# The scan's carried state columns copied by GpSimd instead of ScalarE, in a selective-scan and mixture-of-experts kernel

## The chip, the cores and the metric

One core of a Trainium2 chip runs the kernel. The metric is device time in microseconds for one execution, smaller being better. The engines are named as in the profile: PE (TensorE, with its weight loads as PEld), DVE (VectorE), ACT (ScalarE), POOL (GpSimd) and SP (SyncE, which issues most DMAs). Each engine takes its instructions strictly in the order of its own queue and waits at each one for the semaphores that it needs.

## The reference

Inputs are two sequences of 2048 tokens of 256 numbers, all float32. Everything starts from a layer norm of x. Two branches follow, and their product is added to x:

```python
xn = layernorm(x)
s = mamba_block(xn)            # a selective scan, then an MLP of width 1024
g = silu(moe(xn))              # 8 experts, the top 2 of each token
return x + s * g
```

The part that matters here is the scan. With 512 channels, 16 states per channel, and B and C computed from the input:

```python
def step(h, ts):
    dt_t, B_t, C_t, u_t = ts
    dA = exp(dt_t[..., None] * A)
    h = h * dA + (dt_t * u_t)[..., None] * B_t[:, None, :]
    y = einsum('bds,bs->bd', h, C_t)
    return h, y
```

The state h is carried from each token to the next over the whole sequence.

## The kernel before, in words

The 4096 tokens are cut into 8 blocks of 512; blocks 0 to 3 are the first sequence, 4 to 7 the second. Channels lie on the 128 partitions, in four groups d = 0 to 3, and the 16 states are taken two at a time, g = 0 to 7. So the scan has 256 steps, in the order of block c, group d, pair g; step n is 32c + 8d + g. One step works on tiles of 128 x 2 x 512 and goes through five engines' queues:

- ACT: two exponentials (L1254) make the decays `da` of the step, two steps ahead. `da` has three buffers.
- DVE: for g = 0 the product `du` of the time step and the input (L1358); for each step the product with B (L1361, into PSUM) and two scans over 512 tokens (L1365), one for each state. Their first value is zero in the first block of a sequence and otherwise a column of `hs` of the block before. The scans write `h`, which has five buffers.
- A copy of the last columns of the two scans (128 x 2) into `hs`, for the scan of the next block (`save`, L1291). It is done for blocks 0 to 2 and 4 to 6, 192 steps in all; blocks 3 and 7 end a sequence and save nothing. Before the change ACT does it.
- POOL: the product with C, in place in `h` (L1295), and for most steps the sum of the two states (L1297).
- PE: adds the result into the accumulator `y` in PSUM by a matmul with the identity (L1267), three steps late.

Because L1295 overwrites `h` in place, it has to wait until the copy has read its columns. The loop issues the copy and the product of step n - 1 after the first scan of step n:

```python
if q == 0 and n > 0:
    save(n - 1)
    times_c(n - 1)
exps(n + LEAD, q)
```

`times_c` issues L1295 and L1297, `exps` issues L1254.

All other work is put between the steps by a planner written out in the kernel. `draw` hands out pieces of PE work worth about 2 us for each half step (projections, the next block's front, the experts and, later, the MLP), and a queue of postponed work (`later`) puts the ACT, DVE and POOL instructions that follow from them one or more half steps later. Nothing of it is decided at run time: the order of each engine's queue is fixed when the kernel is built. The parts that come into the prediction's steps are:

- the front of the next block, softplus for a channel group: ACT does L629, L630, L632, L634, L635, POOL subtracts (L636), ACT takes the logarithm (L643), POOL finishes with L648 and L649. In blocks after the first, two groups at a time.
- `root`, for an earlier block's rms norm: POOL L800, ACT L802 and L803, POOL four small operations on 128 x 4 (L227 to L230). It is issued between the two L643 of the first pair of groups.
- the experts: PE matmuls L854 into `phe`, relu on ACT (L954) into `hide`, PE matmuls L866 into `poe`. ACT also copies the transposed rows of the next expert (L846).
- the MLP of finished blocks, from block 5 on: the same matmul lines into `phm` and `pom`, ACT L1018 and L1026, DVE L1028. For its gate POOL gathers expert rows by indirect DMAs (L1058) and adds them (L1076), ACT takes a tanh (L1080), DVE multiplies (L1083, L1101, L1102).
- in block 0 POOL also issues the indirect DMAs that scatter token rows to the experts (L459).

Of the kernel before, what the change touches and what calls it, by code (L numbers as in the profile page):

```python
# [19 lines left out]
T = 512  # L20
# [29 lines left out]
def kernel(  # L50
# [18 lines left out]
    nc = tc.nc  # L69
# [1142 lines left out]
    hs, ys, y_n, hts, das, dus = {}, {}, {}, {}, {}, {}  # L1212
# [75 lines left out]
    def save(n):  # L1288
        c, d, g = at[n]
        if c % CPB != CPB - 1:  # L1290
            nc.scalar.copy(hs[c][:, d, 2 * g : 2 * g + 2], hts[n][:, :, T - 1])  # L1291

    def times_c(n):
        c, d, g = at[n]
# [41 lines left out]
    for n in range(NS):  # L1336
        c, d, g = at[n]
# [14 lines left out]
        for q in range(2):  # L1352
# [17 lines left out]
# [3 lines that stand above are left out]
# [4 lines left out]
            if q == 0:  # L1377

                past = n - BACK
                if past >= 0 and at[past][1] == ND - 1 and at[past][0] + 1 < NBLK:  # L1380
                    load_bc(at[past][0] + 1, at[past][2])
            owed = draw(HALF + owed)
    save(NS - 1)
    times_c(NS - 1)
    for n in range(NS - LAG, NS):
# [64 lines left out]
```

## Time and profile before

| | |
|---|---|
| median of 3 runs | 1550.95 us (1548.26 to 1552.72) |
| the profiled execution | 1551.53 us |
| its span, first to last instruction | 1549.8 us |
| mean granted TensorE clock | 0.948 |
| busy ACT, DVE, POOL | 919.8, 1244.3, 1154.8 us |
| copy L1291 on ACT | 192 of them, 0.188 us each |
| L1295, L1297 on POOL | 2.38 and 1.29 us each |

A row of the profile's groups names line, engine, operation, output and inputs with their shapes, how often, then busy time in us and the mean in ns, and then the idle time of the engine just ahead of these instructions with what ended most of it. The timeline has one row for each instruction or run of equal instructions: start in us from the span's beginning, length, engine, line, and in brackets the idle time ahead of it and what ended it. The first scan of blocks 1 to 4 starts at 272.4, 440.4, 609.5 and 774.

### The profile page before, as it was taken

What the parts mean: (1) busy time and instruction counts of PE and PEld (TensorE: products, weight loads), DVE (VectorE), ACT (ScalarE), POOL (GpSimd) and SP (SyncE); (2) the same over time, 40 slices, a digit from 0 to 9 for tenths busy, and PEclk for the clock granted to TensorE, in tenths of its full rate; (3) what the DMA queues carried; (4) which work ended last, traced back from release to release, by engine and by line L of the source; (5) the groups of instructions that cost most, each with busy time, mean ns of one, the idle gap of its engine ahead of it and who ended that gap; (6) DMA issues with size and microseconds to landing.
All of it is one profiled execution on the core that took longest, in us unless ns stands there. A gap on an engine that the chain in (4) does not pass through costs nothing. (4 is left out here: it accounts for less than half of the span.)

```text
span 1549.8 us, 18158 instructions
## 1 busy us (share of the span) xinstructions
PE 1396.0 (90%) x5246; PEld 982.9 (63%) x5246; DVE 1244.3 (80%) x1362; ACT 919.8 (59%) x1890; POOL 1154.8 (75%) x775
## 2 busy tenths in 40 slices
PE   6747999998999999999999999999888988899667
PEld 4524677666676577667766777667555656667436
DVE  7558887797788977799879777986898788899942
ACT  4846676575656764477557655676465664475322
POOL 2777689768786689679977897688865778677741
PEclk9558999999999999999999999999998999999888
DMA  5594347723592438524853467345610125412100
GB/s 188 206 378 162 94 141 250 268 86 110 165 343 86 129 115 288 199 87 144 271 214 118 129 217 283 92 125 186 225 48 27 49 68 208 131 35 68 55 14 28
DMA packets 171108, 233.70 MB, mean 151 GB/s; under 512 B 19824, under 2 KB 141552, under 8 KB 171008
## 3 DMA queue, kind: packets, MB, share of 16 engines
q1 hardware_dynamic: 164864, 215.75, 42.0%
q0 software_dynamic: 6144, 16.79, 3.2%
q8 instruction: 42, 0.69, 0.2%
q14 instruction: 58, 0.48, 0.1%
HBM read 196.04 MB, written 36.44 MB: 150 GB/s over the span
## 5 line engine op out<-in xcount | busy, mean ns | idle before, releaser
L1295 POOL TENSOR_TENSOR h<-h,C 128x1024 f32<-128x1024 f32 x256 | 608.7, 2379 | 230.9 <-ACT hs L1291 187.4
L1365 DVE TENSOR_TENSOR_SCAN h<-da,hs,b 128x512 f32<-128x512 f32 x384 | 479.0, 1271 | 42.7 <-PE y L1267 17.6
L1254 ACT ACTIVATE da<-dt,a_neg 128x512 f32<-128x512 f32 x512 | 358.2, 718 | 41.6 <-DVE h L1365 41.2
L1267 PE MATMUL y<-h,ident 128*128 128x512 f32 x594 | 304.9, 616 | 32.4 <-POOL h L1295 18.3
L1361 DVE TENSOR_TENSOR b<-du,B 128x1024 f32<-128x1024 f32 x256 | 314.7, 1229 | 19.3 <-DMA B<-bcd 13.3
L854 PE MATMUL phe<-xsTe,w_e 128*128 128x256 f32 x1248 | 290.8, 385 | 13.5 <-ACT hide L954 8.9
L854 PEld LDWEIGHTS phe<-xsTe,w_e 128*128 128x128 f32 x1248 | 239.1, 192 | 81.5 <-issue 25.6
L866 PE MATMUL poe<-w_e,hide 128*128 128x256 f32 x1248 | 289.2, 380 | 0.0
L1297 POOL TENSOR_TENSOR h<-h 128x512 f32<-128x512 f32 x215 | 276.4, 1286 | 16.9
L866 PEld LDWEIGHTS poe<-w_e,hide 128*128 128x128 f32 x1248 | 236.0, 191 | 65.1 <-issue 33.6
L954 ACT ACTIVATE hide<-phe,b 128x256 f32<-128x256 f32 x312 | 129.3, 469 | 129.3 <-PE phe L854 129.1
L1267 PEld LDWEIGHTS y<-h,ident 128*128 128x128 f32 x594 | 112.9, 197 | 122.9 <-issue 66.0
L1365 DVE TENSOR_TENSOR_SCAN h<-da,b 128x512 f32<-128x512 f32 x128 | 151.2, 1210 | 11.2 <-PE y L1267 3.2
L854 PE MATMUL phm<-xsTm,w_m 128*128 128x256 f32 x512 | 125.2, 397 | 21.4 <-DVE hidm L1028 20.8
L854 PEld LDWEIGHTS phm<-xsTm,w_m 128*128 128x128 f32 x512 | 100.6, 198 | 48.9 <-DVE hidm L1028 25.9
L866 PE MATMUL pom<-w_m,hidm 128*128 128x256 f32 x512 | 122.0, 390 | 3.1 <-DVE xom L1102 3.0
L866 PEld LDWEIGHTS pom<-w_m,hidm 128*128 128x128 f32 x512 | 100.0, 197 | 31.8 <-issue 14.4
L1291 ACT COPY hs<-h 128x2 f32<-128x2 f32 x192 | 36.1, 188 | 99.6 <-DVE h L1365 99.4
L459 POOL DMA_INDIRECT xs_d<-xt,slot x64 | 63.3, 989 | 38.7 <-DVE scratch L441 19.8
L1058 POOL DMA_INDIRECT yk<-ys_d,row_y x64 | 61.6, 962 | 38.6 <-DVE pom L1101 21.3
L582 DVE SCALAR_TENSOR_TENSOR xc<-px,par_sb,xc 128x512 f32<-128x512 f32 x96 | 71.5, 746 | 16.6 <-ACT xc L574 11.7
L966 DVE TENSOR_TENSOR ys<-poe,b 128x512 f32<-128x512 f32 x39 | 26.6, 682 | 58.8 <-PE poe L866 51.9
(175 smaller groups left out, 1438.3 us busy)
## 6 DMA issues: line engine op xcount, KB each, us to landing
w_e<-in_w SPq DMA_DIRECT2D x312, 256.0 KB, 3.5
B<-bcd SPq DMA_DIRECT2D x64, 512.0 KB, 6.9
C<-bcd SPq DMA_DIRECT2D x64, 512.0 KB, 7.3
xs<-xs_d SPq DMA_DIRECT2D x39, 256.0 KB, 2.7
ys_d<-ys SPq DMA_DIRECT2D x39, 256.0 KB, 4.2
b<-in_b SPq DMA_DIRECT2D x39, 128.0 KB, 4.1
xnr<-xnd SPq DMA_DIRECT2D x16, 256.0 KB, 7.5
xom<-in_x SPq DMA_DIRECT2D x16, 256.0 KB, 3.3
```

The costliest lines, as they stand in the source:

```text
L459: r = nc.gpsimd.indirect_dma_start(out=xs_d, out_offset=bass.IndirectOffsetOnAxis(ap=slot[:, k, i : i + 1], axis=0), in_=x_of(i // J, i % ...
L582: nc.vector.scalar_tensor_tensor(v[:, s : s + T], px, conv_w[:, d, KC - 1 - s : KC - s], v[:, s : s + T], ALU.mult, ALU.add,)
L854: nc.tensor.matmul(ph[:, q, :], self.w1[c0 // 2][:, k, ts(q, P)], self.xT[:, k, :], start=(k == 0), stop=(k == KM - 1),)
L866: nc.tensor.matmul(po[:, j, :], self.hid[c // 2][:, c % 2, ts(j, P)], self.w2[c // 2][:, c % 2, :], start=(c == 0 and j == 0), stop=(c == ...
L954: nc.scalar.activation(hc[:, q, :], ph[:, q, :], AF.Relu, bias=self.b1[:, c0 + q : c0 + q + 1])
L1058: nc.gpsimd.indirect_dma_start(out=yk[k][:, j, :], out_offset=None, in_=ys_d, in_offset=bass.IndirectOffsetOnAxis(ap=row_y[:, k, i0 + j : ...
L1254: nc.scalar.activation(das[n][:, q, :], dts[c, d], AF.Exp, scale=a_neg[:, d, 2 * g + q : 2 * g + q + 1])
L1267: nc.tensor.matmul(ys[c, d], ident, hts[n][:, q, :], start=False, stop=(g == DS // 2 - 1 and q == nq - 1),)
L1295: nc.gpsimd.tensor_tensor(hts[n], hts[n], bct[c, "C", g], ALU.mult)
L1297: nc.gpsimd.tensor_tensor(hts[n][:, 0, :], hts[n][:, 0, :], hts[n][:, 1, :], ALU.add)
L1361: nc.vector.tensor_tensor(inp, dus[c, d].unsqueeze(1).to_broadcast([P, 2, T]), bct[c, "B", g], ALU.mult,)
L1365: nc.vector.tensor_tensor_scan(hts[n][:, q, :], das[n][:, q, :], inp[:, q, :], 0.0 if c % CPB == 0 else hs[c - 1][:, d, 2 * g + q : 2 * g ...
```

## The change

The copy is issued to GpSimd's queue instead of ScalarE's. Its place in the program is the same, so on POOL it stands directly ahead of the product with C of the same step. Shapes, buffers and everything else stay as they are.

```diff
     def save(n):
         c, d, g = at[n]
         if c % CPB != CPB - 1:
-            nc.scalar.copy(hs[c][:, d, 2 * g : 2 * g + 2], hts[n][:, :, T - 1])
+            nc.gpsimd.tensor_copy(hs[c][:, d, 2 * g : 2 * g + 2], hts[n][:, :, T - 1])
```

In the queues that come out of it, ACT has 192 instructions fewer and POOL 192 more; the orders of PE, DVE and SP are the same. L1291 on POOL waits for DVE's scan, and L1295 waits for L1291 on its own engine, where it waited for ACT's copy before.

## The prediction

> **What bounds the kernel now.** Three rows of the page come first: the engines' busy time, then the groups at the two lines that the change touches.
>
> ```profile
> PE 1396.0 (90%) x5246; PEld 982.9 (63%) x5246; DVE 1244.3 (80%) x1362; ACT 919.8 (59%) x1890; POOL 1154.8 (75%) x775
> ...
> L1295 POOL TENSOR_TENSOR h<-h,C 128x1024 f32<-128x1024 f32 x256 | 608.7, 2379 | 230.9 <-ACT hs L1291 187.4
> ...
> L1291 ACT COPY hs<-h 128x2 f32<-128x2 f32 x192 | 36.1, 188 | 99.6 <-DVE h L1365 99.4
> ```
>
> PE is the bound, so a microsecond counts only where it shortens an idle stretch of PE. POOL stands idle 187.4 us for a copy of 0.19 us: ACT runs in order, the copy sits behind whatever ACT is busy with, and the in-place product of L1295 may not overwrite the state before the copy has read it.
>
> Busy time by stage says how much PE could win. I cut the span at the first scan of each block. PE is idle 9.1 of 168.0 us in block 1, 8.3 of 169.1 in block 2, but 2.2 of 164.5 in block 3, which has no copies (nor has block 7). That is the best hint that the copies cost PE something: 13 us in blocks 1 and 2 if they became like block 3.
>
> The timeline around PE's longest wait of block 1 shows the path (columns: start, length, engine, line; idle time ahead in brackets). ACT first, then POOL, then PE:
>
> ```profile
> 358.13 0.72 ACT L635 ACTIVATE ls<-ls,minus 128x512 f32<-128x512 f32 x1
> 358.76 0.18 ACT L1291 COPY hs<-h 128x2 f32<-128x2 f32 x1
> ...
> 369.05 0.20 ACT L802 ACTIVATE rms<-rms 128x4 f32<-128x4 f32 x1 [4.42 <-POOL rms L800]
> ...
> 370.53 0.82 ACT L954 ACTIVATE hide<-phe,b 128x256 f32<-128x256 f32 x2
> ```
>
> ```profile
> 359.01 2.37 POOL L1295 TENSOR_TENSOR h<-h,C 128x1024 f32<-128x1024 f32 x1 [4.79 <-ACT hs L1291]
> 361.46 1.27 POOL L1297 TENSOR_TENSOR h<-h 128x512 f32<-128x512 f32 x1
> 362.69 2.50 POOL L636 TENSOR_TENSOR ls<-ls,ex 128x512 f32<-128x512 f32 x2
> 365.15 2.34 POOL L1295 TENSOR_TENSOR h<-h,C 128x1024 f32<-128x1024 f32 x1
> 367.58 1.27 POOL L1297 TENSOR_TENSOR h<-h 128x512 f32<-128x512 f32 x1
> 368.81 0.20 POOL L800 TENSOR_SCALAR rms<-rms 128x4 f32<-128x4 f32 x1
> ```
>
> ```profile
> 371.40 3.78 PE L854 MATMUL phe<-xsTe,w_e 128*128 128x256 f32 x8 [4.49 <-ACT hide L954]
> ```
>
> The scan of step 47 (I number steps 0 to 255) ended at 352.00. Its copy waited 6.76 us behind ten softplus instructions of the next block (L629 to L635, 352.51 to 358.85). So POOL idled 4.79 us, brought L800 late, ACT stood 4.42 us before L802, the expert's relu (L954) came late, and PE waited 4.49 us.
>
> **Part 1: the copy leaves ACT.** 192 instructions of 188 ns go. They follow each other closely (358.76 to the next start at 358.84), so each holds ACT up by 0.09 us: 17 us in all, on an engine 59% busy. I count nothing for it. Nor does ACT lose the 99.6 us of waiting for the scan: the next exponential (L1254) writes the buffer that the same scan frees, so it waits for the same event. In blocks 3 and 7 the row of L1254 has this wait (41.2 us).
>
> **Part 2: the copy joins POOL's queue,** directly ahead of L1295, and only that moves; no DMA is issued by it. No row shows a POOL copy of 128x2. The nearest below is the memset of 128x1 (97 ns), the nearest above in shape the 128x4 operations of L227 to L230 (195 to 203 ns); far above, the 128x128 TENSOR_SCALAR of L198 (592 ns). I take 0.20 us, of the nearest shape. The product must wait for the copy on its own engine, as those four wait for each other; they start 0.28 us apart:
>
> ```profile
> 369.57 0.20 POOL L227 TENSOR_TENSOR rms<-rms 128x4 f32<-128x4 f32 x1 [0.56 <-ACT rms L803]
> 369.85 0.20 POOL L228 TENSOR_TENSOR rms<-rms 128x4 f32<-128x4 f32 x1
> 370.15 0.20 POOL L229 TENSOR_SCALAR rms<-rms 128x4 f32<-128x4 f32 x1
> 370.43 0.20 POOL L230 TENSOR_TENSOR rms<-rms 128x4 f32<-128x4 f32 x1
> ```
>
> So 192 x 0.28 = 54 us of POOL, whose share goes from 75% to 78%; the ends are 0.10 and 0.67 us each (19 and 129 us). [...]
>
> Where ACT was prompt the product now starts a little later: before, scan end to copy to product took 0.30 us (step 69: 472.74, 472.77, 473.04); POOL follows a scan directly after 0.13 us (step 102: 649.70, 649.83), so now 0.13 + 0.28 = 0.41. PE reads the state 5 to 10 us after POOL is done in most steps, which hides 0.11 us. Where POOL runs without a gap, each step adds 0.28 us to what is queued behind: the next products, the softplus steps L636 to L649, the gathers L1058 and their sum L1076.
>
> **Part 3: POOL no longer waits for ACT.** I follow POOL's queue from each long wait to the PE wait behind it, letting it stop only for the scan, for ACT's L635 and for its own work.
> - Block 1, 371.40: the product starts at 354.5 instead of 359.0, after L1297's end at 354.23 and the copy. L636 finds both L635 done (355.7, 358.85). With the copy of step 48, L800 comes 4.3 us earlier, ACT can take it (table load over at 362.66): 4.3 of PE's 4.49 us go.
> - Block 1, 411.54 and 424.03: PE waits 0.25 and 2.30 us for L1297. Step 54 had lost 6.29 us to its copy; what is left after three copies is over 5 us ahead: 2.5.
> - Block 2, 542.67: the same pattern (step 79, 4.47 us): L800 3.95 us earlier, all of 3.47. Step 86 (5.25 us): PE's 1.01 at 577.94 and 1.56 at 593.14.
> - Block 6, 1227.41: step 207 had 2.51; PE's 3.40 falls by 2.3. At 1296.57: step 214 had 5.51, but the gather at 1271.96 can come only 1.6 earlier (L1101 ends at 1270.23), less two copies: 1.1. Here DVE is 84% busy and sets much of the pace itself, so I count half of the 3.4: 1.7.
> - Blocks 4 and 5: the POOL waits of PE at 876.21 and 1040.46 have ACT's first L643 in front, so L802 gains 0.6 only, and two copies take 0.56: nothing.
> - Loss: steps 0 to 2, where PE waits for POOL behind the scatters: 3 x 0.28 = 0.8.
>
> Sum: 4.3 + 2.5 + 3.5 + 1.0 + 1.6 + 1.7 - 0.8 = 13.8 us. The profiled execution took 1551.53 us (span 1549.8, 1.7 around it), 0.6 over the median 1550.95. 1551.5 - 13.8 = 1537.7; I forecast **1538**. Late next in blocks 1 and 2 is PE's own work. At 0.10 us a copy the sum is about 15, at 0.67 about 0: the steps ahead of L1297 at 253.79 (step 25, no slack on PE) would end 4 us late, ten copies by 0.39 more, and so would those ahead of steps 154 and 185, which have 0.4 and 0.05 us of slack; with 2 at the start that eats the 13 left.
>
> **Rivals.**
> - *The indirect gains don't arrive.* PE's waits for L954 are then held up by something else on ACT, and only the four waits put down to POOL itself go (0.25 + 2.30 + 1.56 + 0.3 at 1089.42, less 0.8): 3.6 us, 1548. For it: ACT has table loads and exponentials in the same stretch. Against: ACT demonstrably stood idle 4.42 us for L800.
> - *POOL becomes the bound: slower.* Above 0.67 us a copy the sum turns. At 1.05 (a fixed cost like that of a gather's issue, 0.96 + 0.08) ten copies up to step 25 add 10.5 us where 4.4 of waits are saved (+6), the runs in blocks 4 and 5 lose as much (+12), the start 3, and some 8 of the gains are left: +13, 1564. For it: POOL runs gapless over 14 steps in several blocks. Against: every small row of POOL is at 0.2.
> - *DVE is held off by POOL: slower.* The first product of each group (L1358, 128x512) takes 0.67 us at best but 5.09 at 1106.93, just while POOL ran two products without a gap (1106.79 to 1111.46). With L1083 these instructions cost 26.8 us above 0.66 now. If POOL, earlier and fuller, met each of the 33 in question with a whole product (1.7 over 0.66 instead of 0.56), DVE would lose 38 us, half of it hidden in DVE's idle time: +19 - 13.8, 1557. Against: a copy opens a gap of 0.08 us in POOL's run, and DVE got in at such a gap at 191.47. [...]
> - *Blocks 0, 5 and 6 gain as 1 and 2 do,* some 10 us more: 1527.
>
> **Chances.** Forecast 0.54 (own range 1530 to 1546), more gain 0.08, no indirect gain 0.15, POOL bound 0.13, DVE held off 0.10. A measurement can tell 0.3% (4.7 us) from no change here. Faster 0.62, same 0.15, slower 0.23. The range runs from 1527 to 1556: it takes in the copy's dear end (0.67: 1551), most of the DVE rival, and leaves out the bound POOL.
>
> **What would show it.** L1291 as a POOL row of about 0.2 us, 0.28 ahead of L1295; no wait of L1295 for ACT; PE's waits for L954 near steps 47 and 79 gone; blocks 1 and 2 at some 162 and 163 us. Wrong if the copy's spacing is over 0.6, if L1358's mean rises well above 1.2 us, or if PE idles as long in block 1 with other releasers.

## The result and the profile after

The changed kernel took **1527.7 us** (median of 4 runs, 1525.5 to 1529.0) against 1551.8 for the kernel before beside it: ratio 0.9844, 95% interval 0.9831 to 0.9856, 24 us faster. Forecast were 1538 and a range of 1527 to 1556. The profiled execution took 1528.2 us with a span of 1526.5, 23.3 less than before.

The page's busy row, then the groups that answer to those of before (the second is the exponential ahead of which ACT's wait was expected; the copy is the third):

```profile
PE 1388.2 (91%) x5246; PEld 981.3 (64%) x5246; DVE 1245.1 (82%) x1362; ACT 901.4 (59%) x1698; POOL 1191.2 (78%) x967
```

```profile
L1295 POOL TENSOR_TENSOR h<-h,C 128x1024 f32<-128x1024 f32 x256 | 606.2, 2368 | 56.5 <-DVE h L1365 20.9 <-issue 19.7
L1254 ACT ACTIVATE da<-dt,a_neg 128x512 f32<-128x512 f32 x512 | 353.9, 717 | 132.5 <-DVE h L1365 131.9
L1291 POOL COPY hs<-h 128x2 f32<-128x2 f32 x192 | 42.1, 219 | 89.2 <-DVE h L1365 81.2 <-PE po L762 4.6 <-PE phe L854 2.6
```

L1295 no longer waits for ACT: POOL's idle time ahead of it is 56.5 us instead of 230.9. Another 89.2 us now stand ahead of the copy, nearly all of them a wait for the scan itself, so POOL's idle time at the pair fell by 85 us and not by 174. The copy is a POOL row of 0.22 us on average. ACT's wait for the scan has moved to L1254, so ACT itself won nothing but its 18 us of copies. The same row before:

```profile
L1254 ACT ACTIVATE da<-dt,a_neg 128x512 f32<-128x512 f32 x512 | 358.2, 718 | 41.6 <-DVE h L1365 41.2
```

The place of block 1 that the prediction followed, after the change: POOL, then ACT, then PE.

```profile
352.63 0.65 POOL L1291 COPY hs<-h 128x2 f32<-128x2 f32 x1
353.36 2.36 POOL L1295 TENSOR_TENSOR h<-h,C 128x1024 f32<-128x1024 f32 x1
355.80 1.27 POOL L1297 TENSOR_TENSOR h<-h 128x512 f32<-128x512 f32 x1
357.04 1.27 POOL L636 TENSOR_TENSOR ls<-ls,ex 128x512 f32<-128x512 f32 x1
359.34 1.27 POOL L636 TENSOR_TENSOR ls<-ls,ex 128x512 f32<-128x512 f32 x1 [1.03 <-ACT ls L635]
360.56 0.18 POOL L1291 COPY hs<-h 128x2 f32<-128x2 f32 x1
360.82 2.37 POOL L1295 TENSOR_TENSOR h<-h,C 128x1024 f32<-128x1024 f32 x1
363.26 1.27 POOL L1297 TENSOR_TENSOR h<-h 128x512 f32<-128x512 f32 x1
364.50 0.20 POOL L800 TENSOR_SCALAR rms<-rms 128x4 f32<-128x4 f32 x1
```

```profile
358.54 0.72 ACT L635 ACTIVATE ls<-ls,minus 128x512 f32<-128x512 f32 x1
...
364.74 0.20 ACT L802 ACTIVATE rms<-rms 128x4 f32<-128x4 f32 x1 [1.22 <-POOL rms L800]
...
366.22 0.82 ACT L954 ACTIVATE hide<-phe,b 128x256 f32<-128x256 f32 x2
```

```profile
366.30 1.02 PE L1267 MATMUL y<-h,ident 128*128 128x512 f32 x2
367.16 1.92 PE L854 MATMUL phe<-xsTe,w_e 128*128 128x256 f32 x8
```

The product of step 47 starts at 353.36 instead of 359.01, L800 at 364.50 instead of 368.81 (4.31 earlier; 4.3 was forecast), the relu L954 4.31 earlier, and PE takes L854 without a wait. One thing stands there that the forecast did not have: the eight matmuls now last 1.92 us, where the same eight lasted 3.78 behind the wait.

That is the clock. PE's other long wait, in block 2, has the same eight matmuls behind it, before:

```profile
542.67 3.47 PE L854 MATMUL phe<-xsTe,w_e 128*128 128x256 f32 x8 [3.47 <-ACT hide L954]
```

The window view for two stretches of before, and below it for the same places after (columns: stretch, its length, busy time and count of PE, PEld, DVE, ACT, POOL, the granted clock, and last the share and rate of the DMAs):

```profile
369.10:375.70 6.60, 4.30 (x10) 3.50 (x11) 4.88 (x4) 5.47 (x15) 5.72 (x8) 0.50 0.07 24
543.10:546.30 3.20, 3.20 (x9) 2.56 (x8) 3.07 (x3) 2.41 (x7) 3.12 (x4) 0.50 0.00 0
```

```profile
364.60:371.20 6.60, 6.60 (x30) 5.34 (x29) 6.26 (x7) 6.43 (x16) 5.63 (x9) 1.00 0.63 200
530.00:536.00 6.00, 6.00 (x29) 4.98 (x29) 5.80 (x6) 3.89 (x9) 5.76 (x5) 1.00 0.51 157
```

At PE's waits of 4.49 and 3.47 us the clock was granted at half: one record of 6.83 us from 368.96, which is 2.4 us before the end of the first wait, and one of 3.41 us from 543.04, 0.4 us behind the second. After, blocks 1 to 4 have no half-speed record at all.

The span by blocks, cut at the first scan of each. (An error of mine in the section on the profile before: the times given there as first scans of blocks 1 to 3 are those of the second scans of those steps, and the one of block 4 is only approximate. The first scans of blocks 1 to 4 start at 266.7, 439.2, 608.3 and 770.3. The prediction's block lengths go by those marks, too: its 168.0 us for block 1 are 172.5 from first scan to first scan, its 164.5 for block 3 are 161.9; PE's idle times in blocks 1 to 3 are the same by both.)

| stretch | before, us | after, us | PE idle before, after |
|---|---|---|---|
| to the first scan | 87.9 | 87.1 | 26.8, 27.3 |
| block 0 | 178.8 | 180.5 | 27.1, 28.7 |
| block 1 | 172.5 | 163.3 | 9.1, 2.1 |
| block 2 | 169.1 | 160.8 | 8.3, 2.2 |
| block 3 | 161.9 | 160.8 | 2.2, 2.2 |
| block 4 | 162.8 | 162.3 | 3.9, 3.2 |
| block 5 | 180.2 | 177.1 | 11.0, 10.7 |
| block 6 | 206.3 | 203.2 | 25.9, 20.3 |
| block 7 | 166.7 | 168.4 | 22.2, 24.5 |
| behind the last scan | 63.5 | 63.0 | 17.2, 17.0 |

Blocks 1 and 2 bring 17.5 of the 23.3 us.

### The profile page after: what moved, and what is told of

The parts are those of the page before. It is cut to its first block, busy times and chain, and to the rows that moved or that the text cites. A ratio compares the mean times of both kernels' runs of the same rounds, so it can differ in the third digit from the quotient of the medians.

```text
span 1526.5 us, 18200 instructions
## 1 busy us (share of the span) xinstructions
PE 1388.2 (91%) x5246; PEld 981.3 (64%) x5246; DVE 1245.1 (82%) x1362; ACT 901.4 (59%) x1698; POOL 1191.2 (78%) x967
## 5 line engine op out<-in xcount | busy, mean ns | idle before, releaser
L1295 POOL TENSOR_TENSOR h<-h,C 128x1024 f32<-128x1024 f32 x256 | 606.2, 2368 | 56.5 <-DVE h L1365 20.9
L1254 ACT ACTIVATE da<-dt,a_neg 128x512 f32<-128x512 f32 x512 | 353.9, 717 | 132.5 <-DVE h L1365 131.9
L854 PE MATMUL phe<-xsTe,w_e 128*128 128x256 f32 x1248 | 286.4, 381 | 4.3 <-ACT xsTe L846 3.5
L1297 POOL TENSOR_TENSOR h<-h 128x512 f32<-128x512 f32 x215 | 276.3, 1285 | 16.9
L866 PE MATMUL poe<-w_e,hide 128*128 128x256 f32 x1248 | 288.6, 380 | 0.0
L854 PEld LDWEIGHTS phe<-xsTe,w_e 128*128 128x128 f32 x1248 | 237.0, 191 | 70.2 <-issue 27.0
L866 PEld LDWEIGHTS poe<-w_e,hide 128*128 128x128 f32 x1248 | 235.5, 190 | 64.4 <-issue 33.8
L954 ACT ACTIVATE hide<-phe,b 128x256 f32<-128x256 f32 x312 | 129.2, 468 | 134.7 <-PE phe L854 134.2
L854 PE MATMUL phm<-xsTm,w_m 128*128 128x256 f32 x512 | 125.2, 398 | 21.6 <-DVE hidm L1028 20.8
L854 PEld LDWEIGHTS phm<-xsTm,w_m 128*128 128x128 f32 x512 | 100.8, 199 | 49.1 <-DVE hidm L1028 26.5
L866 PE MATMUL pom<-w_m,hidm 128*128 128x256 f32 x512 | 121.2, 388 | 3.0 <-DVE xom L1102 3.0
L866 PEld LDWEIGHTS pom<-w_m,hidm 128*128 128x128 f32 x512 | 99.1, 195 | 30.7 <-issue 13.7
L1291 POOL COPY hs<-h 128x2 f32<-128x2 f32 x192 | 42.1, 219 | 89.2 <-DVE h L1365 81.2
L1026 ACT ACTIVATE hidm<-phm 128x512 f32<-128x512 f32 x64 | 37.6, 593 | 62.6 <-PE phm L854 62.5
```

What stands on the lines that cost most here:

```text
L854: nc.tensor.matmul(ph[:, q, :], self.w1[c0 // 2][:, k, ts(q, P)], self.xT[:, k, :], start=(k == 0), stop=(k == KM - 1),)
L866: nc.tensor.matmul(po[:, j, :], self.hid[c // 2][:, c % 2, ts(j, P)], self.w2[c // 2][:, c % 2, :], start=(c == 0 and j == 0), stop=(c == ...
L954: nc.scalar.activation(hc[:, q, :], ph[:, q, :], AF.Relu, bias=self.b1[:, c0 + q : c0 + q + 1])
L1254: nc.scalar.activation(das[n][:, q, :], dts[c, d], AF.Exp, scale=a_neg[:, d, 2 * g + q : 2 * g + q + 1])
L1295: nc.gpsimd.tensor_tensor(hts[n], hts[n], bct[c, "C", g], ALU.mult)
L1297: nc.gpsimd.tensor_tensor(hts[n][:, 0, :], hts[n][:, 0, :], hts[n][:, 1, :], ALU.add)
```

## The experiments

Theory A is that the wait of POOL's product behind ACT's queue was the cost, made dearer by the half clock behind PE's long waits. Rivals: the copy's place on POOL as such (B), the relief of ACT (C), POOL's own cost (D), the gain spread over all 192 copies (E); the others are named where they come up. The first three edits are to the changed kernel, the others to the kernel before; run 10 has none. The first four kernels ran on a chip where the kernel before takes 1564.3 us (the stretch to the first scan alone is some 14 us longer), so across chips only ratios to the kernel before on the same chip are compared. A gain in microseconds that is given with a ratio is worked out from the ratio. It can differ by 2 or 3 us from the difference of the medians.

**1. The wait put back, POOL's copy kept.** (In this edit and the next two, `junk` is a small tile that is allocated once; that line is left out.)

```diff
+            k = 2 * (n % 8)
             nc.gpsimd.tensor_copy(hs[c][:, d, 2 * g : 2 * g + 2], hts[n][:, :, T - 1])
+            nc.scalar.copy(junk[:, k : k + 2], hts[n][:, :, T - 1])
```

> The changed kernel, and ScalarE also copies the same two columns of the state (to a small buffer that nobody reads), in the place in its order where the kernel before had the copy. So GpSimd pays its copy and its product with C waits for ScalarE's queue again. Theory A (the wait behind ScalarE's queue is what the change took away): the gain goes and GpSimd's copy stays as a cost: 1551 to 1557 us, the row of L1295 again with some 180 us of idle time put down to ScalarE, PE's waits of 4.5 and 3.5 us near steps 47 and 79 back, each with matmuls at half clock behind it. Rival B (what helped is GpSimd's own place in the order, or something else that goes with the copy being on GpSimd): stays within 5 us of 1528.

Measured: 1575.9 us, ratio 1.0078 (1.0060 to 1.0096). The sign is that of theory A, and rival B, which expected most of the gain to stay, is excluded. The loss is larger than expected: 9 to 15 us where at most 6 was expected. Part of that is seen in blocks 1 and 2, which are 3.0 and 4.6 us longer than in the profile of before: they have four half-speed records where that had two. The wait is back and the half clock with it, here on PE near step 47:

```profile
388.45 3.78 PE L855 MATMUL phe<-xsTe,w_e 128*128 128x256 f32 x8 [4.78 <-ACT hide L955]
```

The profile puts POOL's idle time ahead of the product mostly down to "issue" here (119.1 of 167.2 us), since the product waits for both copies; that ACT's copy ends last is seen in the timeline, where the product starts 0.3 us after that copy's start (375.83, 375.52).

**2. ACT's load put back, without the wait.**

```diff
+            nc.scalar.copy(junk[:, k : k + 2], zero3[:, 0:2])
```

> The changed kernel, and ScalarE makes a copy of the same size from a constant to a small buffer that nobody reads, in the old place in its order: its load is back, the wait that ties GpSimd's product to it is not. Theory A (the wait): 1528 to 1531 us, L1295 without idle time put down to ScalarE's copy. Rival C (the relief of ScalarE, 192 instructions at 0.09 us of queue each, 17 us, which I counted as nothing): a good part of the 24 us comes back, 1535 to 1545.

Measured: 1543.6 us, ratio 0.9867 (0.9848 to 0.9887). Most of the gain stays; against the changed kernel's 0.9844 and 0.9846 on other chips it is some 3 us dearer, with intervals that overlap. Rival C is refuted as the cause. Blocks 1 and 2 last 164.5 and 160.8 us, PE idles 2.1 and 2.3 us in them, and the page shows their clock at 0.9 or more in every slice. The groups of the product and of ACT's copy:

```profile
L1298 POOL TENSOR_TENSOR h<-h,C 128x1024 f32<-128x1024 f32 x256 | 606.7, 2370 | 57.1 <-DVE h L1368 20.7 <-issue 20.2
L1294 ACT COPY junk<-zero 128x2 f32<-128x2 f32 x192 | 35.6, 185 | 0.0
```

192 copies on ACT, and L1298 (the product) waits no more than in the changed kernel.

**3. A second copy on POOL.**

```diff
+            nc.gpsimd.tensor_copy(junk[:, k : k + 2], hts[n][:, :, T - 1])
```

> The changed kernel with a second GpSimd copy of the same two columns (to a small buffer that nobody reads) between the copy and the product. It doubles what the copy costs GpSimd, about 0.28 us a step, so GpSimd goes from 78% to about 80 or 81% busy. By the terms of my sum a copy costs PE the 0.28 us at the three start steps, about 0.8, and little elsewhere while slack lasts: 1529 to 1533 us. Rival D (GpSimd is near to being the bound, each step's queue passes the delay on): 10 steps of each busy run pass it on, 192 x 0.28 = 54 us at the very most, 1540 or more.

Measured: 1548.3 us, ratio 0.9891 (0.9871 to 0.9911), 4.7 us over kernel 2 on the same chip and some 7 over the changed kernel by the ratios. The second row has 0.188 us a copy, but the edit does not double the cost on POOL as was expected. The second copy waits for nothing and starts 0.12 us (median) behind the start of the first, while the product still starts 0.265 us behind the copy ahead of it. In sum the time from the first copy's start to the product's rises from 57.5 us in the changed kernel to 79.5, and POOL's busy time from 1191.2 to 1213.5 us (78%). So some 22 us more of POOL's queue cost 5 to 7 us of the whole: more than the start steps alone, but a quarter to a third of what rival D's argument, that the queue passes every delay on, would make of them.

**4. No copy at all.**

```diff
-            nc.gpsimd.tensor_copy(hs[c][:, d, 2 * g : 2 * g + 2], hts[n][:, :, T - 1])
+            pass
```

> The changed kernel without any copy: the carry from each block into the next block's scan is left out, each block starts from zeros that are written once at allocation. The time says what is still to be had from the copy. If the copies cost PE only the start steps and a few places: 1522 to 1528 us. If GpSimd's queue passes on every copy in its busy runs (rival D): 1518 or less.

(A second part of the edit, which sets `hs` to zero once for each block, is left out here.) Measured: 1535.5 us, ratio 0.9815 (0.9798 to 0.9831), some 4.6 us under the changed kernel by the ratios. That is what the copy still costs on balance, since it also spares VectorE a wait at the end of block 5 that is back without it (see below).

**5. POOL copies in blocks 1 and 2 alone.**

```diff
-            nc.scalar.copy(hs[c][:, d, 2 * g : 2 * g + 2], hts[n][:, :, T - 1])
+            copy = nc.gpsimd.tensor_copy if c in (1, 2) else nc.scalar.copy
+            copy(hs[c][:, d, 2 * g : 2 * g + 2], hts[n][:, :, T - 1])
```

> The kernel before with the copy on GpSimd in blocks 1 and 2 alone; in blocks 0, 4, 5 and 6 ScalarE copies as before. Theory A, with the places as the two traces show them (blocks 1 and 2 shorter by 9.2 and 8.3 us, blocks 5 and 6 by 3.1 each, block 0 longer by 1.7): 17 to 18 us of the 24 come, 1533 to 1535 on a chip where the kernel before takes 1551, ratio 0.988 to 0.989. My forecast's own terms for these blocks, without the half clock behind PE's waits, were 12.9: ratio 0.9917. Rival E (the gain is spread over all copies, as a relief of ScalarE would be): half of the copies, half of the gain, ratio 0.992.

Measured: 1532.5 us, ratio 0.9873 (0.9847 to 0.9899), a gain of 19.7 us (16 to 24). Both my forecast's own 12.9 us (0.9917) and the even spread of rival E (0.992) lie outside the interval. The other 128 copies are worth some 4 us by the ratios, but the interval overlaps with the changed kernel's, so that is not clear of noise.

**6. POOL copies at steps 47 and 79 alone** (the same edit with `n in (47, 79)`).

> The kernel before with GpSimd's copy at two steps alone, 47 and 79 (numbered as 32 x block + 8 x d + g), which stand ahead of PE's longest waits of blocks 1 and 2 (4.49 and 3.47 us); the other 190 copies stay on ScalarE. My forecast for these two: 4.3 + 3.5 = 7.8 us, ratio 0.9950. With the half clock that followed those two waits (the first eight matmuls took 3.78 and 3.47 us instead of some 1.95 and 1.9): 3.5 us more, 11 us, ratio 0.9928, and the clock records at full speed from 370 to 376 and from 543 to 547. Rival E: 2 of 192 copies, nothing.

Measured: 1539.7 us, ratio 0.9914 (0.9894 to 0.9934), a gain of 13.4 us (10 to 16; the medians differ by 10.9). The 0.9950 without the clock lies outside the interval, the 0.9928 with it inside. So two copies of 192 bring about half of the gain. There is no half-speed record in blocks 1 and 2, and in the profile they are 6.6 and 5.4 us shorter than before: the two waits with their slow matmuls make 6.35 and 5.05.

**7. The clock by itself:** the kernel before, with TensorE kept busy in its two waits. (The lines that hand this bank on to the expert's own product are left out.)

```diff
+                fill = {39: 9, 67: 6}.get(pairs[0], 0)
+                pairs[0] += 1
+                if fill:
+                    got = bank("o", [P, JS, DM], f"po{self.name}")
+                    held.append(self.name)
+                    for _ in range(fill):
+                        nc.tensor.matmul(
+                            got[0][:, 0, :], ident, in_sb[:, 0, 0:DM], start=True, stop=True
+                        )
                 self.pair(c0)
```

> The kernel before, copies on ScalarE, nothing moved on VectorE, ScalarE and GpSimd. TensorE gets filler matmuls in its two longest waits of blocks 1 and 2 (nine of them at 371.40, some 3.9 us of 4.49; six at 542.67, some 2.6 of 3.47): their result goes to the expert's output bank and is overwritten by that expert's first real product. They shorten no wait, they only keep TensorE busy in it. Theory A (half of those blocks' surplus over my forecast is the clock that a long wait of TensorE pulls down): no half clock near 370 and 543, the eight matmuls behind each wait at some 1.9 us instead of 3.78 and 3.47, blocks 1 and 2 shorter by some 1.7 us each, ratio 0.998. Rival H (the clock falls there for another reason, or the matmuls were slow for another reason): those eight still take 3.5 us, the blocks as long as before or longer, ratio 1.000 or more.

Measured: ratio 0.9962 (0.9950 to 0.9974). PE at the first place (L893 is the filler, L855 the expert's matmul):

```profile
370.06 4.05 PE L893 MATMUL poe<-in_sb,ident 128*128 128x256 f32 x18
374.70 2.00 PE L855 MATMUL phe<-xsTe,w_e 128*128 128x256 f32 x8 [0.59 <-ACT hide L967]
```

and at the second:

```profile
541.86 2.75 PE L893 MATMUL poe<-in_sb,ident 128*128 128x256 f32 x12
545.49 2.00 PE L855 MATMUL phe<-xsTe,w_e 128*128 128x256 f32 x8 [0.88 <-ACT hide L967]
```

The relu that they wait for comes no earlier, yet the eight matmuls take 2.00 us instead of 3.78 and 3.47, with the clock granted at 1.00 (372.0 to 378.6 and 544.0 to 548.0). So at these two places the half clock follows from PE standing idle, and it cost 1.8 + 1.5 us. Blocks 1 and 2 are 1.2 and 0.9 us shorter, less than the 1.7 each expected. In block 1 a part was lost again: the clock fell to half at 425.67, behind a wait for L1297 of 2.28 us. The kernel before has the same wait, 2.30 us, with no half clock. The matmuls L866 (L867 in this run) behind it, before and in this run:

```profile
425.00 1.89 PE L866 MATMUL poe<-w_e,hide 128*128 128x256 f32 x8
426.56 3.14 PE L867 MATMUL poe<-w_e,hide 128*128 128x256 f32 x8
```

The time as a whole fell by 4.0 to 7.8 us by the ratio (4.4 between the medians), more than the 3.4 expected; the profile has 4.5 us in block 6, which this edit does not touch and which varies (below), so the surplus is not explained.

**8. The copy on VectorE** (`nc.vector.tensor_copy` in place of `nc.scalar.copy`).

> The copy on VectorE, directly behind its own scan, so that GpSimd neither waits for ScalarE nor pays. VectorE is 82% busy and gets 192 more instructions of some 0.1 to 0.2 us (no row shows this one): 19 to 40 us of VectorE. Theory A (the wait behind ScalarE is the whole cause, and PE has slack for VectorE in blocks 0 to 4): as fast as the changed kernel or a little faster in blocks 0 to 4, slower in blocks 5 and 6, where VectorE sets the pace: ratio 0.980 to 0.990. Rival F (only GpSimd's place helps): near 1.

Measured: 1541.7 us, ratio 0.9927 (0.9904 to 0.9949), a miss: less gain than expected, though more than rival F's none. Two things were overlooked, and both are in the trace; how much each costs was not measured apart. `save(n - 1)` is issued behind the first scan of step n, so on DVE the copy comes a whole scan (1.27 us) after the state is done. And the copy is long at many places: 0.14 us at best, 0.39 on average, over 0.5 in 43 of 192 and 2.2 at worst. DVE, then POOL, at one of these:

```profile
372.33 1.28 DVE L1365 TENSOR_TENSOR_SCAN h<-da,hs,b 128x512 f32<-128x512 f32 x1
373.53 1.87 DVE L1291 COPY hs<-h 128x2 f32<-128x2 f32 x1
375.32 1.27 DVE L1365 TENSOR_TENSOR_SCAN h<-da,hs,b 128x512 f32<-128x512 f32 x1
```

```profile
373.02 2.36 POOL L1295 TENSOR_TENSOR h<-h,C 128x1024 f32<-128x1024 f32 x1
```

The copy ends when POOL's product does (375.40 and 375.38); the next scan comes right behind.

**9. ACT's copy, issued earlier:** behind the second scan of its own step.

```diff
+            if q == 1:
+                save(n)
             if q == 0 and n > 0:
-                save(n - 1)
                 times_c(n - 1)
```

> The kernel before, copy still on ScalarE, but issued right after the second scan of its own step instead of half a step later, so that fewer instructions of ScalarE stand between the scan and the copy; ScalarE then waits for the scan itself before it goes on to the next block's softplus. Theory A (what costs is how long the copy stands behind other work in ScalarE's queue): GpSimd's wait falls, but ScalarE's own work comes later: some part of the gain, ratio 0.985 to 1.00, with the row of L1295 well under 187 us for ScalarE. Rival G (any copy on ScalarE costs, wherever it stands): 1.00 or more.

(The last `save` behind the loop goes, too.) Measured: 1566.0 us, ratio 1.0084 (1.0060 to 1.0107), slower than any expectation but that of rival G, by which any copy on ACT costs:

```profile
L1295 POOL TENSOR_TENSOR h<-h,C 128x1024 f32<-128x1024 f32 x256 | 609.4, 2382 | 212.4 <-ACT hs L1291 166.0 <-issue 23.3 <-DVE h L1365 21.0
L1291 ACT COPY hs<-h 128x2 f32<-128x2 f32 x192 | 36.7, 191 | 225.6 <-DVE h L1365 225.4
```

POOL's wait for ACT hardly fell (166.0 us from 187.4), while ACT now waits 225.4 us for the scan, 99.4 before, with its softplus queued behind. An in-order queue that holds both a copy waiting for the scan and work that others wait for is late for one or the other. It is the waiting that costs and not a copy on ACT as such: run 2 has 192 of them there, which wait for no scan and which nobody waits for, at a cost of some 3 us.

**10 and 11. The changed kernel again, and with ACT's copy in block 0,** side by side.

```diff
+            copy = nc.gpsimd.tensor_copy if c else nc.scalar.copy
+            copy(hs[c][:, d, 2 * g : 2 * g + 2], hts[n][:, :, T - 1])
```

> The changed kernel once more, so that the next one stands beside it on one chip, and so that it is seen which blocks' lengths repeat: ratio 0.983 to 0.987. Blocks 1 and 2 at 163 and 161 us again; the small differences of blocks 0, 5 and 6 (+1.7, -3.1, -3.1) may not repeat, since block 0 was 178.8 to 184.1 us and block 6 202 to 207 us long in kernels that do the same there.

> The changed kernel, but with the copy on ScalarE in block 0, where GpSimd's copy was counted as a loss of 0.8 us and the trace after shows PE's waits for GpSimd's products at the start longer by 1.6. If that loss is real: 1 to 2 us under the changed kernel, ratio to it 0.999. If block 0's waits behind ScalarE cost PE more than that: equal or slower.

Measured: 1527.6 us, ratio 0.9846 (0.9832 to 0.9861), and 1531.4, ratio 0.9859 (0.9845 to 0.9873). The result repeats. ACT's copy in block 0 is no better, although 1 to 2 us were hoped for, so no kernel tried here that does the whole work beats the changed one.

## Why the prediction was right, and where it was not

The sign and the mechanism were right, but the size was not: 13.8 us of gain were forecast, 24 came, 23.3 of them in the profile.

- **Block 1, 371.40 (4.3 forecast).** The wait went whole, 4.49 us, by the path described. Missing was a term: the eight matmuls behind it lost 1.86 us to the half clock.
- **Block 1, 411.54 and 424.03 (2.5).** Both waits gone, 2.55 us. With the two above the block's terms come to 8.9; its length fell by 9.2.
- **Block 2 (3.5 + 1.0 + 1.6).** All three waits gone, 6.04 us, and 1.6 more at half clock; the length fell by 8.3.
- **The step that failed in blocks 1 and 2 is therefore the price of a PE wait:** I counted a removed wait at its length alone. Two of the waits cost some 40% more than their length, 11.4 instead of 8.0 us together. That is 3.4 of the 9.5 us by which the profile's gain exceeds my sum; another 3.1 are block 5 (below), and the rest, some 3 us in small pieces of both signs, is not explained. Runs 6 and 7 show it from both sides: with the waits gone at these two steps, and with the waits left and the clock held. The half clock stood in the trace of before, in the clock records and in those 3.78 us beside a normal 1.9, and I had not looked. It was no accident of the two: of 70 PE waits as long as these, 3.4 us or more, between 240 and 1450 us in thirteen traces of this study, 68 had half clock set in during them or no later than 2 us after their end. But shorter waits are not safe: of 46 between 1.8 and 2.5 us, 18 had it, too. The wait of 2.30 us at 424.03 had none, the same one in run 7 did; that it cost no more than its length in the kernel before was luck.
- **Block 6 (1.7).** Not confirmed. PE's idle time fell there (25.9 to 20.3 us), but the block is 203.2 and 204.4 us long in the two runs of the changed kernel, and 201.7 to 202.7 in runs 5, 6 and 7, where ACT copies in it as before. The 206.3 of before's profile was at the upper end of what this block takes anyway.
- **Blocks 4 and 5 (nothing).** Block 4: right, 0.5. Block 5 became shorter by 3.1 (and by 4.8 in the repeat), most likely for a reason that I had as a rival with the opposite sign; see the next point. It repeats: block 5 lasts 175.4 to 177.1 us in five traces with POOL's copy alone and 180.2 to 180.3 in four with ACT's copy as before. Blocks 5 and 6 together are 380.3 and 379.8 us after, 386.5 before, but 381.9 to 383.0 in runs 5 to 7, with ACT's copy there, and 383.3 in run 11, with POOL's: whether anything of it lasts beyond block 6 stays open.
- **DVE held off by POOL (rival, slower).** L1358 and L1083 all but keep their cost (29 us above 0.66 each, 27 before), and L1358's mean goes from 1.22 to 1.25 us. L1358 loses 1.8 us more in each of blocks 1 and 2, hidden there: PE idles only 2.1 and 2.2 us in them. But the longest, 5.09 us at the end of block 5, fell to 0.69. POOL, then DVE, before:

```profile
1106.79 4.67 POOL L1295 TENSOR_TENSOR h<-h,C 128x1024 f32<-128x1024 f32 x2
```

```profile
1106.93 5.09 DVE L1358 TENSOR_TENSOR du<-dt,xc 128x512 f32<-128x512 f32 x1
```

and after:

```profile
1089.80 0.19 POOL L1291 COPY hs<-h 128x2 f32<-128x2 f32 x1
1090.07 2.71 POOL L1295 TENSOR_TENSOR h<-h,C 128x1024 f32<-128x1024 f32 x1
1092.74 0.18 POOL L1291 COPY hs<-h 128x2 f32<-128x2 f32 x1
```

```profile
1089.89 0.69 DVE L1358 TENSOR_TENSOR du<-dt,xc 128x512 f32<-128x512 f32 x1
```

  Before, two products ran without a gap there (4.67 us, to 1111.46) and L1358 ended 0.56 us behind both (1112.02). Now a copy stands ahead of each; L1358 starts beside the first copy and ends at 1090.58, 0.51 us into the product, and the product is longer (2.71 instead of 2.36). L1358 takes 0.69 there in every kernel with POOL's copy in block 5, and 5.08 to 5.17 in every one with ACT's copy as before or with none (runs 4 to 7).
- **The copy's cost (0.20 busy, 0.28 apart, 0.8 us in all).** The median is 0.185 us and the spacing 0.26 to 0.28 (360.56 to 360.82); the mean is raised by copies that last up to 0.73 us (0.65 at 352.63; all 14 of the 192 over 0.23 us lie beside DVE's L1358 or L1083). The cost to the whole was put too low: it is 4.6 us by run 4, and 5 to 7 for a second copy by run 3. Of the 0.8 at the start, PE's wait for L1295 near 120 us shows 0.2 to 1.0 (9.05 to 9.76 us with POOL's copy, 8.71 to 8.84 with ACT's in its old place, in nine traces), but block 0 lasts 178.9 to 181.7 us with POOL's copy and 178.8 to 184.1 with ACT's there, so no loss can be told.
- **ACT's relief (nothing).** Right by run 2, up to some 3 us. ACT's wait moved to L1254 as said.
- **POOL as the bound, no indirect gain.** Neither came: the waits for L954 went with the waits for L800, and PE idles 2.1 us in block 1.
- **Block lengths as a sign (162 and 163 us).** By the prediction's own marks, the second scans, blocks 1 and 2 came to 159.3 and 160.8.
- **The range** held the time with 0.7 us to spare. That was in part luck: the forecast's own range of 1530 to 1546 did not hold it, and more gain had a chance of 0.08. The rival "blocks 0, 5 and 6 gain too" gave the right number (1527) for reasons that are right in part at most: block 0 gained nothing, block 6 nothing that can be told from what it varies by, block 5 did, and 3.4 us came from the clock in blocks 1 and 2.

## What to carry to other kernels

When an in-place consumer waits only for a small reader, put that reader on the consumer's own queue, if that queue has a few per cent to spare (POOL went from 75% to 78% here): it then waits for what it needs and not for what stands ahead of the reader elsewhere. Price a TensorE wait as long as the two here, 3.4 us or more (half clock at 68 of 70), at its length plus the slow matmuls behind it, expect them now and then behind one of 1.8 to 2.5 us, too (18 of 46), and read the granted clock in that stretch before summing. Compare the lengths of untouched stretches over several traces before calling a change of 3 us there a gain.

## What the runs showed of the hardware that was not expected

- Half clock lasted 6.8 us at a single wait of 4.49 us in block 1 and 3.4 us at one of 3.47 in block 2, all but 2.4 us of it while PE was busy again; with filler matmuls in the waits the clock was granted at 1.00 there (run 7). A wait of 2.3 us at one and the same place had half clock behind it in run 7's trace and not in that of before.
- VectorE's copy of 128x2 took 0.14 us at best and 2.2 at worst (run 8). One of 1.87 us ran from 373.53 to 375.40, beside a product of GpSimd that ended at 375.38; what held it was not shown.
- With a short GpSimd instruction ahead of each of two long ones, VectorE's L1358 took 0.69 us where it had taken 5.09 (end of block 5).
